# A four-layer graph network on one core: one ScalarE tile in the first groups, two sign buffers, projections one tile later, and other entries into layers 2 and 3

## The chip, the cores and the metric

The kernel runs on one core of a Trainium2 chip. A core has TensorE (PE, matmul), VectorE (DVE), ScalarE (ACT), GpSimd (POOL) and SyncE (SP), which here only issues transfers, and 16 DMA engines. The metric is the device time of one execution in microseconds; the times are medians of several runs of the same program.

## The reference

The network has 3327 nodes with 256 features and four layers, each applied as x = x + layer(relu(layernorm(x))) with a dense 3327 x 3327 matrix `adj` of which about 1% is set, the diagonal included.

```python
# layer 0, two steps n
R = S + eye; R = R / R.sum(-1)            # S = adj
A = top_p_attention(Xa, W1, W2, W3)       # softmax(q k^T), keep the largest 0.9 of each row
Xf = R @ Xf
Xa = A @ Xa
Z = Z + Xf @ U1[n].T + Xa @ U2[n].T       # at the end layernorm(X + Z)
# layer 1
filt = tanh(adj * adj) * (adj > 0)        # the 700 largest of each row
feat = relu(filt @ (tanh(h @ W_proj) @ W_gcn))
# layers 2 and 3
e = leaky_relu(Wh @ a1 + (Wh @ a2).T)     # masked by adj > 0 (layer 2: or the diagonal)
h = softmax(e) @ Wh                       # layer 3 ends in elu
```

## The kernel before, in words

The nodes are padded to 26 tiles of 128 rows. Everything is in 32-bit floats and stays on the core, apart from rows that go out to DRAM and come back.

**Layer 0** runs from 0 to about 2010 us, in two steps `s`, the second from about 1022 us. A step takes its 26 tiles in groups of three (`group`). A group makes the scores of its tiles (L1042), brings them out of PSUM on VectorE (L1016) and takes their exponentials on ScalarE (L1025). Then it looks for the threshold of the top 0.9 of each row in four rounds `r`: each round sums what lies above the present guess over the whole row of 3328 scores. A tile in `on_act` has that sum made by two ScalarE passes (L1126, Relu and Sign into the scratch tile `junk_a`), every other tile by one VectorE pass (L1131); `ON_ACT = [2, 2, 1, 2]` says how many of a group's three tiles are ScalarE's in each round. At the end of a round some ten small VectorE instructions (from L1137) make the next guess, for all three tiles at once, from both engines' sums. After the rounds each tile has three more passes (L1173, L1176, L1187). The group's tiles then go to `weighted`, which turns the kept scores with PE transposes (L951), copies them out on ScalarE (L953), multiplies them with Xa (L941), loads the tile's row of Xf as `xf_in` (L935), turns both rows (L785) and multiplies them with U1 and U2 (L971). `neighbours` makes the row R @ Xf of a tile: four blocks of the turned adjacency are loaded (`blk`, L906), in step 0 their signs are taken on ScalarE into `sg` (L909) and stored for layers 2 and 3 (`sign_d`, L910), and 26 matmuls follow (L915, two records each). Its result goes out through `xf_row` (L923, L924).

`group`, `weighted` and `neighbours` are generators. `overlapped` starts a group every 20 ticks and runs one stage of each generator per tick, so that about two groups and several tiles are in work together.

**Layer 1** (to 2343 us) goes tile by tile: two halves of the turned adjacency are loaded into one of three pairs of places, filtered on VectorE (L1478) and ScalarE (L1479), and multiplied (L1482). For the tile before, `summed` adds the result to x and takes its statistics; for the tile before that, `tile_in` makes the input of layer 2: the normed row `hr` (ScalarE, L1400), its two PE transposes (L785) with a copy `ht` (ScalarE, L786), the projection (PE, L1405) and its copies `sd` and `wh` (ScalarE, L1409 and L1410). After the last tile of a span of four, `spread` lays the source terms over all partitions (L1422, L1425) and takes maxima over the first span's positions (VectorE, L1429). Positions `pos` of the set elements are found from the rows of `adj` (L1496) and stored (`pos_d`).

**Layers 2 and 3** (`attention`, 2343 to 2731 and 2731 to 3099 us) go by spans of four tiles, the last of two. For pairs of column tiles, ScalarE makes two exponentials (L1585, L1586), VectorE combines and masks them (L1587, L1588), and PE multiplies (L1594). Statistics, `tile_in` and `spread` of the next layer stand in a list `todo`; from the second block of a span on, each block takes one entry of it. What is left after the last span is done at its end, then the next layer begins with `scores_of` (L1534, L1541).

All transfers are issued by SP in one order. The order of every engine's instructions is fixed when the program is built: it follows the order in which the code above emits them, with instructions whose operands are expected earlier moved ahead. At run time each engine takes its list in order, and an instruction at the head of it waits for its operands and for the release of the buffer that it writes. A tile with `bufs=1` has one buffer; without `bufs`, its pool's default of two.

Of the kernel before, what the change touches and what calls it, by code (L numbers as in the profile page):

```python
# [9 lines left out]
F32 = mybir.dt.float32  # L10
BF16 = mybir.dt.bfloat16
I32 = mybir.dt.int32
U8 = mybir.dt.uint8
I8 = mybir.dt.int8
AF = mybir.ActivationFunctionType
ALU = mybir.AluOpType
# [4 lines left out]
P = 128  # L21
N = 3327
NT = 26
NP = NT * P
LAST = N - (NT - 1) * P
D = 256
# [8 lines left out]
ON_ACT = [2, 2, 1, 2]  # L35
# [31 lines left out]
def kernel(  # L67
# [23 lines left out]
    nc = tc.nc  # L91
# [649 lines left out]
    spans = [list(range(i, min(i + 4, NT))) for i in range(0, NT, 4)]  # L741
# [4 lines left out]
    def layers(fast):  # L746
# [54 lines left out]
        def layer0(wp, mp, ap_, tp, sp):  # L801
# [97 lines left out]
            def neighbours(s, it, xf):  # L899
# [3 lines left out]
                for chunks in QB:  # L903
# [3 lines left out]
                    if s == 0:  # L907
                        sg = tp.tile([P, 7, P], I8, tag="sg", bufs=1, name="sg")
                        nc.scalar.activation(sg[:, :n, :], blk[:, :n, :], AF.Sign)  # L909
                        nc.sync.dma_start(sign_d[it, :, chunks[0] : chunks[0] + n, :], sg[:, :n, :])  # L910
# [16 lines left out]
            def weighted(s, it, e, norm, xa, xa_next, us):  # L927
# [3 lines left out]
                else:  # L931
                    base = tp.tile([P, D], F32, tag="base", bufs=1, name="base_row")
                    nc.sync.dma_start(base, zz_d[it * P : (it + 1) * P, :])
                xf_in = tp.tile([P, D], F32, tag="xf_in", name="xf_in")
                nc.sync.dma_start(xf_in, (xf_d, xf2_d)[s][it * P : (it + 1) * P, :])  # L935
# [65 lines left out]
            def group(s, tiles, xa, xf, xa_next, us, slots, products_of, also):  # L1001
# [113 lines left out]
                for r in range(ROUNDS):  # L1115
                    on_act = list(range(max(g - ON_ACT[r], g - 2 if g > 2 else 1), g)) if g > 1 else []
                    A = slice(on_act[0], g) if on_act else None
# [241 lines left out]
        class Entry:  # L1359
# [5 lines left out]
            def __init__(self, name, w, wh, dk_tag, eye):  # L1365
                self.w, self.wh, self.eye, self.mv = w, wh, eye, {}
                for t in wh.halves:
# [3 lines left out]
                self.dk = slot(dk_tag, [P, NP], f"dk{name}")  # L1371
                self.tops = late.tile([P, 4, len(spans)], F32, name=f"tops{name}")
                sq = late.tile([P, 2], F32, tag="sq", name="sq")
                nc.vector.tensor_tensor(sq, w[:, :, D + 1], w[:, :, D + 1], ALU.mult)
                ps = ps_row()
                nc.tensor.matmul(ps[:, :2], ones, sq, start=True, stop=True)
                self.shift = late.tile([P, 1], F32, name=f"shift{name}")
                self.low = late.tile([P, 1], F32, name=f"low{name}")
                shift = self.shift
# [5 lines left out]
                nc.gpsimd.tensor_scalar(self.low, shift, -1.0 + 2.0**-20, None, ALU.mult)  # L1385
                if not eye:

                    self.part = late.tile([P, D + 1], F32, name="part")
                    nc.gpsimd.memset(self.part, 0.0)

# [5 lines left out]

            def tile_in(self, it, src):
                hr = late.tile([P, D], F32, tag="hr", bufs=2, name="hr")
                mv = self.mv.pop(it)
                nc.scalar.activation(hr, src, AF.Relu, bias=mv[:, 0:1], scale=mv[:, 1:2])  # L1400
                ht = late.tile([P, D], F32, tag="ht", bufs=2, name="ht")
                transposed(hr, ht)
                ps = ps_row()
# [48 lines left out]
        entry2 = Entry("2", w2l, nodes(("a0", "a1"), D + 2, "wh2"), "bl", True)  # L1452
        with tc.tile_pool(name="l1", bufs=2, reuse_waits="tile") as l1:
            third = l1.tile([P, 2, HB * P], F32, bufs=1, name="blk1_2")
            places = [[places[n][:, k, :] for n in range(2)] for k in range(2)] + [[third[:, n, :] for n in range(2)]]
# [7 lines left out]

            def entered2(it):
                entry2.tile_in(it, xn(it))
                if it in ends:
                    entry2.spread(ends.index(it))

            for it in range(NT):
# [3 lines left out]
                for hb in range(2):  # L1473
                    filt = places[it % 3][hb]
                    nc.sync.dma_start(
# [9 lines left out]
                if it >= 1:  # L1485
                    summed(it - 1)
                if it >= 2:
                    entered2(it - 2)
                ar = slot(f"e{it % 2}", [P, NP], "adj_rows")
# [3 lines left out]
                for a, b in rows_to_load(it):  # L1493
                    nc.sync.dma_start(ar[a:b, :N], adj[it * P + a : it * P + b, :])
                pos = pos_first[:, it, :] if it in spans[0] else l1.tile([P, NP], U8, tag="pos", name="pos")
                nc.vector.tensor_scalar(  # L1496
# [4 lines left out]
            summed(NT - 1)  # L1501
            entered2(NT - 2)
            entered2(NT - 1)


# [10 lines left out]
        def attention(entry, finish, following=None):  # L1516
# [33 lines left out]
            for i, span in enumerate(spans):  # L1550
# [16 lines left out]
                for b, j0 in enumerate(range(0, NT, JB)):  # L1567
# [30 lines left out]
                    if 1 <= b <= len(ahead):  # L1598
# [6 lines left out]
                        if b == len(ahead):  # L1605
                            sb_next = scores_of(ahead, top)
                    if b and todo:
                        for work in todo.pop(0):
                            work()
# [10 lines left out]
                if following is not None:  # L1620

                    stats = [lambda it=it: following.stats(it, xn(it)) for it in span]
                    rest = [lambda it=it: following.tile_in(it, xn(it)) for it in span]
                    todo += [stats[:2]] + [rest[k : k + 1] + stats[k + 2 : k + 3] for k in range(n)]
                    todo.append([lambda i=i: following.spread(i)])
            for works in todo:
# [108 lines left out]
```

## Time and profile before

The median of three runs is 3104.74 us (3103.69 to 3111.75).

| | us |
|---|---|
| profiled execution, its own time | 3100.91 |
| its span | 3099.1 |
| PE busy | 2823.0 (91%) |
| PE weight loads busy | 2277.8 (73%) |
| VectorE busy | 2370.4 (76%) |
| ScalarE busy | 1979.7 (64%) |
| GpSimd busy | 417.8 (13%) |
| chain of work that ended last | DVE 38%, PE 27%, ACT 16%, issue 8%, DMA 7%, POOL 3% |

The span is the part of the execution that the profiler sees. Busy times of the engines overlap, so they don't add up to it. A line of the profile names an engine, a line of the code (L1126), and output and input; "<-" ahead of another instruction names what ended an idle time. The line numbers are those of the kernel before.

### The profile page before, as it was taken

Reading aid. Unit: us, or ns where it says so; the run is one execution under the profiler, and the core shown is the slowest. Engines: PE = TensorE matmul, PEld = TensorE weight load, DVE = VectorE, ACT = ScalarE, POOL = GpSimd, SP = SyncE. Lnnn points to the kernel's source line nnn. Section 1 sums busy time; section 2 is a strip of 40 time slices with the busy share of each in tenths; the row PEclk is TensorE's granted clock in tenths of the full one; section 3 lists DMA queues with packets and bytes.
Section 4 is the critical chain, followed back from the end, with each engine's and each line's share of the span. In section 5 each row is a group of like instructions: output and inputs, shape, how many; then the busy total and the mean of one; then the engine's idle time right before and its main releaser. Section 6 shows DMA issues by size and latency. Waiting matters only on the chain.

```text
span 3099.1 us, 37681 instructions
## 1 busy us (share of the span) xinstructions
PE 2823.0 (91%) x13454; PEld 2277.8 (73%) x13454; DVE 2370.4 (76%) x4133; ACT 1979.7 (64%) x2633; POOL 417.8 (13%) x742
## 2 busy tenths in 40 slices
PE   7788899999999899999999988999997999979998
PEld 5466677777778576667777767888886887758887
DVE  3678889778874588889876858377765999769996
ACT  6767787768773566687666555433334777657776
POOL 0120010000001001111110024211110333210000
PEclk9889999999999999999999989999998999989999
DMA  4431112321242231211232231388871211112221
GB/s 138 131 102 45 55 45 76 95 78 57 75 121 87 73 103 53 64 35 54 74 90 72 83 114 60 105 321 318 324 243 32 71 59 59 30 48 78 75 74 37
DMA packets 183035, 298.83 MB, mean 96 GB/s; under 512 B 24701, under 2 KB 137016, under 8 KB 179512
## 3 DMA queue, kind: packets, MB, share of 16 engines
q1 hardware_dynamic: 182838, 296.34, 30.3%
q8 instruction: 108, 1.77, 0.3%
q14 instruction: 89, 0.72, 0.1%
HBM read 251.97 MB, written 44.30 MB: 96 GB/s over the span
## 4 chain that ended last, share of the span: by engine, by line
DVE 38%; PE 27%; ACT 16%; issue 8%; DMA 7%; POOL 3%; SPq 0%; ACTq 0%; POOLq 0%; DVEq 0%
ACT junk_a L1126 9%; PE ps_wide L1594 5%; DVE below L1173 4%; PE ps_out L941 4%; PE ps_acc L915 4%; DVE w L1176 4%; PE ps_wide L1482 4%; DVE below L1131 3%; DVE e L1187 3%; DVE places L1601 3%; DVE places L1587 2%; DVE below L1085 2%; DVE places L1588 2%; DMA blk<-in_adj_t 2%; DMA adj_rows<-in_adj 2%
## 5 line engine op out<-in xcount | busy, mean ns | idle before, releaser
L1126 ACT ACTIVATE junk_a<-e,minus 128x3328 int8<-128x3328 f32 x208 | 638.8, 3071 | 3.7
L1594 PE MATMUL ps_wide<-wh,places 128*128 128x257 f32 x1872 | 451.2, 383 | 35.6 <-DVE places L1588 32.7
L1594 PEld LDWEIGHTS ps_wide<-wh,places 128*128 128x128 f32 x1872 | 353.3, 191 | 93.6 <-ACT places L1586 16.5
L915 PE MATMUL ps_acc<-h,blk 128*128 128x258 f32 x1352 | 333.3, 399 | 46.8 <-ACT xf_row L923 37.1
L915 PEld LDWEIGHTS ps_acc<-h,blk 128*128 128x128 f32 x1352 | 261.8, 198 | 102.3 <-ACT xf_row L923 42.7
L1016 DVE TENSOR_SCALAR_CACHE_REDUCE e<-ps_wide 128x1024 f32<-128x1024 f32 (+1 forms) x176 | 178.6, 1019 | 206.9 <-PE ps_wide L1042 206.4
L915 PE MATMUL ps_acc<-xf,blk 128*128 128x256 f32 x1352 | 312.9, 384 | 14.3 <-ACT xf_row L923 14.2
L941 PE MATMUL ps_out<-h,wt 128*128 128x256 f32 x1352 | 311.2, 381 | 4.7 <-ACT wt L953 4.7
L941 PE MATMUL ps_out<-xa,wt 128*128 128x256 f32 x1352 | 311.9, 381 | 0.9 <-ACT wt L953 0.7
L1585 ACT ACTIVATE places<-places,sd 128x512 f32<-128x512 f32 (+1 forms) x364 | 246.3, 684 | 100.5 <-PE ps_wide L1594 67.6
L1482 PE MATMUL ps_wide<-gw,blk 128*128 128x256 f32 x1352 | 300.9, 379 | 1.3 <-ACT blk L1479 1.3
L915 PEld LDWEIGHTS ps_acc<-xf,blk 128*128 128x128 f32 x1352 | 253.9, 191 | 61.8 <-ACT xf_row L923 19.3
L1482 PEld LDWEIGHTS ps_wide<-gw,blk 128*128 128x128 f32 x1352 | 254.5, 190 | 35.0 <-ACT blk L1479 1.7
L941 PEld LDWEIGHTS ps_out<-h,wt 128*128 128x128 f32 x1352 | 249.8, 190 | 40.1 <-ACT wt L953 6.3
L941 PEld LDWEIGHTS ps_out<-xa,wt 128*128 128x128 f32 x1352 | 249.4, 190 | 34.8 <-ACT wt L953 3.0
L1586 ACT ACTIVATE places<-places,d 128x512 f32<-128x512 f32 (+1 forms) x364 | 235.8, 682 | 48.7 <-DVE places L1587 48.2
L1131 DVE SCALAR_TENSOR_TENSOR below<-e,v 128x3328 f32<-128x3328 f32 x72 | 265.3, 3684 | 1.8
L1587 DVE TENSOR_TENSOR places<-places,places 128x1024 f32<-128x1024 f32 (+1 forms) x182 | 210.2, 1163 | 65.8 <-ACT places L1585 63.7
L1042 PE MATMUL ps_wide<-keys,q 64*128 64x512 f32 (+1 forms) x832 | 215.9, 570 | 17.8 <-DVE e L1016 14.8
L953 ACT COPY wt<-ps_wide 128x1024 f32<-128x1024 f32 x208 | 175.2, 846 | 86.2 <-PE ps_wide L951 85.6
L1588 DVE SCALAR_TENSOR_TENSOR places<-blk_s,places 128x1024 f32<-128x1024 int8 (+1 forms) x182 | 206.3, 1142 | 2.0
L1176 DVE MAX8 w<-below 128x8 f32<-128x3328 f32 x52 | 188.3, 3621 | 0.3
(275 smaller groups left out, 4312.6 us busy)
## 6 DMA issues: line engine op xcount, KB each, us to landing
blk<-in_adj_t SPq DMA_DIRECT2D x104, 448.0 KB, 3.5
blk<-in_adj_t SPq DMA_DIRECT2D x52, 832.0 KB, 7.1
adj_rows<-in_adj SPq DMA_DIRECT2D x25, 1663.5 KB, 8.4
blk<-in_adj_t SPq DMA_DIRECT2D x104, 384.0 KB, 3.3
blk_s<-sign_d SPq DMA_DIRECT2D x72, 256.0 KB, 2.9
blk_s<-pos_d SPq DMA_DIRECT2D x44, 416.0 KB, 3.6
pos_d<-pos SPq DMA_DIRECT2D x22, 416.0 KB, 2.9
xf_d<-xf_row SPq DMA_DIRECT2D x52, 128.0 KB, 2.4
```

What stands on the lines that cost most here:

```text
L915: nc.tensor.matmul(acc[:, :w], blk[:, j, :], xf(jc)[:, :w], start=(jc == 0), stop=(jc == NT - 1))
L941: nc.tensor.matmul(po, wt[:, k * P : (k + 1) * P], xa(jc)[:, :D], start=(jc == 0), stop=(jc == NT - 1))
L1042: nc.tensor.matmul(pl[:, f * 512 : f * 512 + cw], q[f * DA : (f + 1) * DA, :], kt[f * DA : (f + 1) * DA, s, c0 : c0 + cw], start=True, sto ...
L1126: nc.scalar.activation(junk, es[i], (AF.Relu, AF.Sign)[n], bias=minus[:, 0, i : i + 1], accum_out=(ga, sa)[n][:, 0, i : i + 1],)
L1131: nc.vector.scalar_tensor_tensor(below, es[i], v[:, 3, i : i + 1], es[i], ALU.is_ge, ALU.mult, accum_out=v[:, 1, i : i + 1],)
L1176: nc.vector.max(w9[:, i, 1:9], below)
L1482: nc.tensor.matmul(po, filt[:, j * P : (j + 1) * P], gw(jc), start=(jc == 0), stop=(jc == NT - 1))
L1585: nc.scalar.activation(e1[:, :, q, :], s0, AF.Exp, bias=sd[:, jc + q, 1:2])
L1586: nc.scalar.activation(e2[:, :, q, :], s1, AF.Exp, bias=d2[:, jc + q : jc + q + 1])
L1587: nc.vector.tensor_tensor(e1, e1, e2, ALU.max)
L1588: nc.vector.scalar_tensor_tensor(e1, signs[:, :n, j : j + 2, :], 0.0, e1, ALU.is_gt, ALU.min)
L1594: nc.tensor.matmul(pos_[k], e1[:, k, q, :], wh(jc + q)[:, : D + 1], start=(jc + q == 0), stop=(eye and jc + q == NT - 1),)
```

## The change

1. `sg` gets two buffers, `xf_in` one instead of two.
2. In the group that holds tile 0, which is the first of each step, one tile is ScalarE's in every round instead of `ON_ACT[r]`.
3. The bound `shift` of an `Entry` is no longer computed when the entry is made but by `shifted`, called in the third tile of layer 1 and in the second span of layer 2.
4. `tile_in` becomes `turned` (norm, transposes, copy) and `projected` (matmul and copies, `spread` after it); in both callers `projected` comes one tile later than `turned`. At the end of layer 1 the last tiles are made with less distance from the sum that they follow.
5. In `attention`, the last span takes two entries of `todo` in every block, the first included.
6. In layer 1 the three pairs of places are taken in turn from the second on, and the two `pos` tiles are named and chosen by `it % 2`.

```diff
@@ -905,7 +905,7 @@
                     blk = ap_.tile([P, 7, P], F32, tag="blk", name="blk")
                     nc.sync.dma_start(blk[:, :n, :], adj_t[it, :, chunks[0] : chunks[0] + n, :])
                     if s == 0:
-                        sg = tp.tile([P, 7, P], I8, tag="sg", bufs=1, name="sg")
+                        sg = tp.tile([P, 7, P], I8, tag="sg", name="sg")
                         nc.scalar.activation(sg[:, :n, :], blk[:, :n, :], AF.Sign)
                         nc.sync.dma_start(sign_d[it, :, chunks[0] : chunks[0] + n, :], sg[:, :n, :])
                     if it in chunks:
@@ -931,7 +931,7 @@
                 else:
                     base = tp.tile([P, D], F32, tag="base", bufs=1, name="base_row")
                     nc.sync.dma_start(base, zz_d[it * P : (it + 1) * P, :])
-                xf_in = tp.tile([P, D], F32, tag="xf_in", name="xf_in")
+                xf_in = tp.tile([P, D], F32, tag="xf_in", bufs=1, name="xf_in")
                 nc.sync.dma_start(xf_in, (xf_d, xf2_d)[s][it * P : (it + 1) * P, :])
                 po = ps_out0()[:, :D]
 
@@ -1113,7 +1113,9 @@
                 todo = list(products_of)
                 first = 2 if g == len(todo) else 0
                 for r in range(ROUNDS):
-                    on_act = list(range(max(g - ON_ACT[r], g - 2 if g > 2 else 1), g)) if g > 1 else []
+
+                    most = 1 if tiles[0] == 0 else ON_ACT[r]
+                    on_act = list(range(max(g - most, g - 2 if g > 2 else 1), g)) if g > 1 else []
                     A = slice(on_act[0], g) if on_act else None
                     if on_act:
                         nc.scalar.mul(minus[:, 0, A], v[:, 3, A], -1.0)
@@ -1363,19 +1365,25 @@
 
 
             def __init__(self, name, w, wh, dk_tag, eye):
-                self.w, self.wh, self.eye, self.mv = w, wh, eye, {}
+                self.w, self.wh, self.eye, self.mv, self.ht = w, wh, eye, {}, {}
                 for t in wh.halves:
                     nc.gpsimd.memset(t[:, :, D : D + 1], 1.0)
                 self.sd = late.tile([P, NT, 2], F32, name=f"sd{name}")
                 self.d2 = late.tile([P, NT], F32, name=f"d2{name}")
                 self.dk = slot(dk_tag, [P, NP], f"dk{name}")
                 self.tops = late.tile([P, 4, len(spans)], F32, name=f"tops{name}")
+                self.shift = late.tile([P, 1], F32, name=f"shift{name}")
+                self.low = late.tile([P, 1], F32, name=f"low{name}")
+                if not eye:
+
+                    self.part = late.tile([P, D + 1], F32, name="part")
+                    nc.gpsimd.memset(self.part, 0.0)
+
+            def shifted(self):
                 sq = late.tile([P, 2], F32, tag="sq", name="sq")
-                nc.vector.tensor_tensor(sq, w[:, :, D + 1], w[:, :, D + 1], ALU.mult)
+                nc.vector.tensor_tensor(sq, self.w[:, :, D + 1], self.w[:, :, D + 1], ALU.mult)
                 ps = ps_row()
                 nc.tensor.matmul(ps[:, :2], ones, sq, start=True, stop=True)
-                self.shift = late.tile([P, 1], F32, name=f"shift{name}")
-                self.low = late.tile([P, 1], F32, name=f"low{name}")
                 shift = self.shift
                 nc.vector.tensor_reduce(shift, ps[:, :2], AX.X, ALU.add)
                 nc.gpsimd.tensor_scalar(shift, shift, 1.01 * D, EPS, ALU.mult, ALU.add)
@@ -1383,10 +1391,6 @@
                 nc.gpsimd.tensor_scalar(shift, shift, 1.0, None, ALU.add)
 
                 nc.gpsimd.tensor_scalar(self.low, shift, -1.0 + 2.0**-20, None, ALU.mult)
-                if not eye:
-
-                    self.part = late.tile([P, D + 1], F32, name="part")
-                    nc.gpsimd.memset(self.part, 0.0)
 
             def stats(self, it, src):
 
@@ -1394,12 +1398,15 @@
                 nc.gpsimd.tensor_scalar(mv[:, 0:1], mv[:, 0:1], mv[:, 1:2], -1.0, ALU.mult, ALU.mult)
                 self.mv[it] = mv
 
-            def tile_in(self, it, src):
+            def turned(self, it, src):
                 hr = late.tile([P, D], F32, tag="hr", bufs=2, name="hr")
                 mv = self.mv.pop(it)
                 nc.scalar.activation(hr, src, AF.Relu, bias=mv[:, 0:1], scale=mv[:, 1:2])
-                ht = late.tile([P, D], F32, tag="ht", bufs=2, name="ht")
-                transposed(hr, ht)
+                self.ht[it] = late.tile([P, D], F32, tag="ht", bufs=2, name="ht")
+                transposed(hr, self.ht[it])
+
+            def projected(self, it):
+                ht = self.ht.pop(it)
                 ps = ps_row()
                 for c in range(2):
                     nc.tensor.matmul(
@@ -1451,6 +1458,8 @@
         places = [slot(f"e{4 + n}", [P, 2, HB * P], f"blk1_{n}") for n in range(2)]
         entry2 = Entry("2", w2l, nodes(("a0", "a1"), D + 2, "wh2"), "bl", True)
         with tc.tile_pool(name="l1", bufs=2, reuse_waits="tile") as l1:
+
+            pos_places = [l1.tile([P, NP], U8, bufs=1, name=f"pos{n}") for n in range(2)]
             third = l1.tile([P, 2, HB * P], F32, bufs=1, name="blk1_2")
             places = [[places[n][:, k, :] for n in range(2)] for k in range(2)] + [[third[:, n, :] for n in range(2)]]
             po_of = {}
@@ -1461,8 +1470,8 @@
                 nc.vector.scalar_tensor_tensor(xn(it), pre, 0.0, xs(it), ALU.max, ALU.add)
                 entry2.stats(it, xn(it))
 
-            def entered2(it):
-                entry2.tile_in(it, xn(it))
+            def projected(it):
+                entry2.projected(it)
                 if it in ends:
                     entry2.spread(ends.index(it))
 
@@ -1471,7 +1480,7 @@
                     po2 = ps_wide()
                 po = po_of[it] = po2[:, 512 * (it % 2) : 512 * (it % 2) + D]
                 for hb in range(2):
-                    filt = places[it % 3][hb]
+                    filt = places[(it + 1) % 3][hb]
                     nc.sync.dma_start(
                         filt, adj_t[it, :, hb * HB : (hb + 1) * HB, :].rearrange("p j i -> p (j i)")
                     )
@@ -1484,23 +1493,31 @@
                         )
                 if it >= 1:
                     summed(it - 1)
-                if it >= 2:
-                    entered2(it - 2)
+
+                for k in range(it - 2 if it < NT - 1 else it - 1, it - 1 if it < NT - 2 else it):
+                    if k >= 0:
+                        entry2.turned(k, xn(k))
+                if it == 2:
+                    entry2.shifted()
+                for k in range(it - 3 if it < NT - 1 else it - 2, it - 2 if it < NT - 2 else it - 1):
+                    if k >= 0:
+                        projected(k)
                 ar = slot(f"e{it % 2}", [P, NP], "adj_rows")
                 r = rows_of(it)
                 if r < P:
                     nc.vector.memset(ar, 0.0)
                 for a, b in rows_to_load(it):
                     nc.sync.dma_start(ar[a:b, :N], adj[it * P + a : it * P + b, :])
-                pos = pos_first[:, it, :] if it in spans[0] else l1.tile([P, NP], U8, tag="pos", name="pos")
+                pos = pos_first[:, it, :] if it in spans[0] else pos_places[it % 2]
                 nc.vector.tensor_scalar(
                     pos[:, :N], ar[:, :N], 0.0, None, ALU.is_gt, ALU.add, accum_out=counts[:, it : it + 1]
                 )
                 nc.gpsimd.memset(pos[:, N:], 0)
                 nc.sync.dma_start(pos_d[it], pos)
             summed(NT - 1)
-            entered2(NT - 2)
-            entered2(NT - 1)
+            projected(NT - 2)
+            entry2.turned(NT - 1, xn(NT - 1))
+            projected(NT - 1)
 
 
         att = fast.enter_context(tc.tile_pool(name="att", bufs=1, reuse_waits="tile"))
@@ -1604,8 +1621,10 @@
                         )
                         if b == len(ahead):
                             sb_next = scores_of(ahead, top)
-                    if b and todo:
-                        for work in todo.pop(0):
+                    if following is not None and (i, b) == (1, 1):
+                        following.shifted()
+                    for _ in range(2 if ahead == [] else 1 if b else 0):
+                        for work in todo.pop(0) if todo else []:
                             work()
                 for k, it in enumerate(span):
                     if not eye:
@@ -1620,9 +1639,12 @@
                 if following is not None:
 
                     stats = [lambda it=it: following.stats(it, xn(it)) for it in span]
-                    rest = [lambda it=it: following.tile_in(it, xn(it)) for it in span]
-                    todo += [stats[:2]] + [rest[k : k + 1] + stats[k + 2 : k + 3] for k in range(n)]
-                    todo.append([lambda i=i: following.spread(i)])
+                    turned = [lambda it=it: following.turned(it, xn(it)) for it in span]
+                    made = [lambda it=it: following.projected(it) for it in span]
+                    todo += [stats[:2]] + [
+                        turned[k : k + 1] + made[max(k - 1, 0) : k] + stats[k + 2 : k + 3] for k in range(n)
+                    ]
+                    todo.append(made[-1:] + [lambda i=i: following.spread(i)])
             for works in todo:
                 for work in works:
                     work()
```

## The prediction

> **What bounds the kernel now.** I read the page's engine totals, then busy time by stretches, then the waits of the stretches that are not full, and last the timeline around each place that the diff touches.
>
> ```profile
> PE 2823.0 (91%) x13454; PEld 2277.8 (73%) x13454; DVE 2370.4 (76%) x4133; ACT 1979.7 (64%) x2633; POOL 417.8 (13%) x742
> ```
>
> TensorE's matmul work is the same before and after the change, so at an unchanged clock (mean 0.973) a gain can come only out of its 3099.1 - 2823.0 = 276 us of idle time. Where that idle time lies is seen in stretches: width, then busy us of PE, weight loads, DVE, ACT and POOL, then PE's clock, the DMA share and GB/s.
>
> ```profile
> 100.00:150.00 50.00, 36.99 (x142) 26.83 (x141) 24.07 (x76) 40.63 (x34) 8.97 (x16) 0.86 0.52 151
> 150.00:200.00 50.00, 34.58 (x138) 27.90 (x138) 37.71 (x62) 28.77 (x27) 19.94 (x15) 0.83 0.49 147
> 250.00:300.00 50.00, 41.63 (x197) 31.44 (x196) 37.96 (x89) 34.50 (x38) 1.63 (x10) 0.93 0.17 49
> 1050.00:1100.00 50.00, 44.12 (x189) 33.65 (x187) 32.18 (x91) 42.21 (x33) 3.14 (x8) 0.93 0.42 119
> 2010.00:2343.00 333.00, 319.85 (x1507) 276.19 (x1506) 226.87 (x265) 111.86 (x154) 53.24 (x109) 1.00 0.79 288
> ```
>
> From 100 to 200 PE idles 28.4 us, from 1050 to 1100 it idles 5.9; layer 1 (2010 to 2343) has 13.2 us. At both starts of layer 0's steps ACT is the busiest engine after PE, and DVE has room. The timeline of DVE in the first group's second round shows why (start, duration, and in brackets the idle time before it):
>
> ```profile
> 133.02 3.69 DVE L1131 SCALAR_TENSOR_TENSOR below<-e,v 128x3328 f32<-128x3328 f32 x1
> ...
> 148.08 0.16 DVE L1137 SCALAR_TENSOR_TENSOR sa<-sa,v 128x2 f32<-128x2 f32 x1 [10.77 <-ACT junk_a L1126]
> ...
> 150.38 3.69 DVE L1131 SCALAR_TENSOR_TENSOR below<-e,v 128x3328 f32<-128x3328 f32 x1
> ```
>
> DVE makes one pass over one tile and then waits 10.8 us for ACT, which makes two passes for each of two tiles. The waits of the whole run, and those of PE within layer 1, hold the two other targets (total us, times, longest):
>
> ```profile
> ACT sg L909 <- DMA sign_d<-sg: 54.9, 23, 5.4
> SPq L935 <- PE ps_row L785: 152.7, 28, 18.0
> ```
>
> ```profile
> PE ps_row L1405 <- ACT ht L786: 10.6, 10, 2.6
> PE ps_row L1422 <- ACT sd L1409: 1.3, 1, 1.3
> PE ps_wide L1482 <- ACT blk L1479: 1.3, 1, 1.3
> ```
>
> **What the Trainium skill says.** "Perfetto Trace Analysis", Optimization Strategy: look for the gaps on the engine that should be saturated, stretch by stretch; repeated equal gaps can mean too few buffers. The trace agrees as to layer 1 (ten like gaps), though their cause is an order, not a buffer. "ScalarE: Activation LUTs", What ACT_TABLE_LOAD costs: an ACTIVATE with a pointer bias takes about 280 ns + 0.833 ns an element; for 3328 that is 3.05 us, and the trace has 3.07. So ACT's pair costs 2 x (3.07 + 0.19 read) = 6.5 us a tile, DVE's one pass 3.69 + 0.08. "TensorE: Matmul & The Clock Gate", What's actually happening: an array idle for some 3.4 us falls to half clock. Agreed: the four records of the projection L1405 take 2.09 us at 2350.76, after a gap, and 1.14 in the shadow at 2344.01.
>
> **Part 1, one ACT tile in the first group of each step.** Of rounds r0, r1, r3 one tile goes from ACT to DVE: ACT loses 3 x 6.5 = 19.5 us, DVE gains 3 x 3.8 = 11.3. Round r2 has that split already and is the price. In step 0 the rounds last 26.2, 17.4, 9.9 and 17.2 us (starts of L1131 at 106.8, 133.0, 150.4, 160.3, end 177.5); r1 and r3 fall to about 9.9, r0, held by the exponentials of its third tile, by some 5: 7.4 + 7.3 + 5 = 20 us. In step 1 they last 18.0, 15.9, 9.1, 15.4: r0 gives some 3 (DVE waits there for PE's L1042 until 1069.1, and for ACT only 2.6), so 6.8 + 6.3 + 3 = 16 us. The first weighted products start that much sooner. But PE doesn't save it all: in the built order, of the neighbour products (L915, rows of 333.3 and 312.9 us, so 646.2 / 52 = 12.4 us a tile) 6.3 tiles stood before the first weighted tile and now 5.0; in step 1 32.3 and now 31.2. So 1.3 x 12.4 = 16 and 1.1 x 12.4 = 14 us of PE work move behind it and are caught up after nine more weighted tiles. From 200 to 500 PE idles 28.6 us (by 50 us: 4.9, 8.4, 2.9, 6.7, 2.9, 2.8) and can take some of it for nothing. I let 40% of the moved work be hidden: -20 + 0.6 x 16 = **-10.4** in step 0, -16 + 0.6 x 14 = **-7.6** in step 1. Ends: all hidden -20 and -16, none -4 and -2. The cover of DVE's added 11 us is its waits for ACT (6.3, 10.8 and 2.3 us in r0, r1, r3 of step 0, the last one beside 8.6 us more ended by PE); without it 11 us a step would come back.
>
> **Part 2, two sign buffers, one xf_in.** The second sg buffer takes away up to 54.9 us of ACT waits, 18.3 of these between 60 and 200 us. PE waits for blk copies through POOL there (4.7 us), else hardly at all: **-2**, ends 0 and -5. The single xf_in makes each load (L935, 2.0 us to landing, 3.8 at most) wait for the transpose (L785) of the tile before instead of the one before that. The load moves one tile later in SP's list, so SP stands at the same release as now (152.7 us over 28 loads), and neighbour blocks, q and base loads behind it are held no longer. Transposes of successive tiles are at 563.8, 611.9, 636.7, 669.2, 716.6: at least 24.8 us apart, against 2.0 + SP's 5.5 mean wait. **0**, ends 0 and +8 (a miss of 3.8 us at a couple of tiles).
>
> **Part 3, projection one tile after the transpose in layers 1 and 2.** In layer 1, PE's 10.6 us behind ht copies go, since PE now uses the copy of the tile before. Next could be DMA: 2 x 832 + 1663.5 + 416 KB a tile is 3.83 MB per 333/26 = 12.8 us, 299 GB/s, and the page reaches 324, good for 11.8 us; DVE (68% busy) isn't near. **-8**, ends 0 and -10.6. With the step its ACT copies (sd L1409 0.16, wh L1410 0.38, dk L1425 0.69 us) and, for a span's last tile, L1422 and four L1429 passes on DVE also come a tile later; none of them has a reader before attention starts. It issues no DMA. In layer 2's attention PE waits 3.9 us for ht; DVE, the bound there (PE waits 17.0 us for its L1588), keeps half: **-2**, ends 0 and -4. The order of the pos and filter buffers and the moved shift chain (one 0.59 us matmul, L1376, and a few small DVE and POOL ones) are hidden by the matmul stretch into which they go: **0**, and +3 if layer 1's first filter load were late.
>
> **Part 4, the two entries.** PE's timeline between layers 1 and 2:
>
> ```profile
> 2343.09 0.38 PE L785 MATMUL ps_row<-ident,hr 128*128 128x128 f32 x2
> 2344.01 1.14 PE L1405 MATMUL ps_row<-w2l,ht 128*128 128x258 f32 x4 [0.53 <-ACT ht L786]
> 2344.98 0.73 PE L1422 MATMUL ps_row<-ident,sd 128*128 128x128 f32 x4
> 2349.13 0.44 PE L785 MATMUL ps_row<-ident,hr 128*128 128x128 f32 x2 [3.41 <-ACT hr L1400]
> 2350.76 2.09 PE L1405 MATMUL ps_row<-w2l,ht 128*128 128x258 f32 x4 [1.19 <-ACT ht L786]
> 2352.64 0.63 PE L785 MATMUL ps_row<-ident,hr 128*128 128x128 f32 x2
> ```
>
> Tile 23's projection and spread run in the shadow of tile 24's statistics. In the new order they stand behind tile 24's transpose at 2349.13: 2.09 cold + 0.73 to 1.5, in place of the 1.19 us wait for ht, so tile 24's projection starts at about 2352.3, not 2350.8; tile 25's wait of 0.53 goes. **+1.5**, ends 0 and +3. Between layers 2 and 3 the spread of the sixth span leaves the tail: four L1429 passes from 2732.15 to 2734.60, 2.5 us on DVE ahead of the statistics, and about 0.6 us of ht waits. Against that, two works a block in the last span put transposes and projections close together on PE, which may wait for ACT copies of 0.4 to 1.2 us there, 1 to 3 in all: **-1**, ends -3 and +2.
>
> **Sum.** -10.4 - 7.6 - 2 + 0 - 8 - 2 + 0 + 1.5 - 1 = -29.5 us. The profiled execution took 3100.9 us (span 3099.1 and 1.8 around it), 3.8 below the median of 3104.7. I take the difference to the median: **3075 us**.
>
> **Rivals.** *A, the start gain is handed back*: PE is the bound from 200 on (46 to 48 of 50), all the moved neighbour tiles are paid for: -4 - 2 at the starts, -1 for the sign buffer, -5 in layer 1 and nothing at the entries: 3104.7 - 12 = about 3093. For it: the 95% PE of 500 to 1000 (473.9 of 500); against it: 200 to 450. *B, no measurable change*: layer 1 is held by DMA at a share of 0.79 (0.74 to 0.88) so that its gaps reappear as waits for filters, and A as well: -8 + 1.5, with +2 to +6 at small places, 3100 to 3104. *C, slower*: the one xf_in buffer holds SP's in-order list. If a load waits longer than now, the neighbour blocks behind it come late, and PE's L915 starves. 29.5 us over 52 loads is 0.57 us, and it decides from there on; at 1 us a load the sum is -29.5 + 52 = +22, 3127. For it: SP waits up to 18.0 us at this line already; against it: the 24.8 us spacing and the load's later place. *D, the change does nothing at the start*, because r0 is bound by the third tile's exponentials: its gain is only 5 of 20, so this costs no more than A.
>
> **Chances.** Forecast 0.63 (its own range 3056 to 3088), A 0.15, B and smaller sums 0.12, C 0.10. The forecast and A are faster, with a few of C's mild cases and B's better ones in the middle: faster by more than 0.3% (9 us, about what a measurement of this kernel tells from none) 0.77, within 0.13, slower 0.10. For 8 in 10 the range takes the forecast down to all-hidden starts, A, and part of B: 3053 to 3103.
>
> **What would show it.** First group of step 0: DVE's idle before L1137 for ACT falls from 10.8 to under 1, rounds of about 10 us, the first L951 some 20 us earlier; step 0's end earlier by half of that. ACT's sg wait near 0; SP's wait at L935 about 150. In layer 1, no PE wait for ht, and a stretch of 325 instead of 333. Transition gaps of 27.4 (2343.3 to 2370.7) and 30 us (2730.5 to 2760.6) become 29 and 29. It is wrong if PE waits for neighbour blocks more than now, if DVE's wait moves to L1016 in rounds, or if PE's granted clock drops below 0.97 as it fills up.

## The result, and the profile after

The changed kernel takes 3089.28 us (median of 7 runs, 3087.01 to 3094.23), the kernel before beside it 3104.8 (7 runs, 3101.63 to 3111.75). The ratio is 0.9946, its 95% interval [0.9935, 0.9956] (given in brackets from here on): about 16 us faster, where 29.5 had been forecast. The same program, taken once more in the last set of experiments, gave 3096.72 (6 runs, 3084.47 to 3097.98) and 0.9969 [0.9953, 0.9985]. The two intervals share only gains of 13.7 to 14.6 us, and between the two sets of runs the size is 8 to 16 us: it is known no better than that.

The engine totals of the changed kernel:

```profile
span 3086.7 us, 37714 instructions
PE 2824.4 (92%) x13454; PEld 2287.4 (74%) x13454; DVE 2394.5 (78%) x4145; ACT 1942.3 (63%) x2609; POOL 400.4 (13%) x742
```

ScalarE has lost 37 us and VectorE gained 24, while PE's work is as it was. The span is 12.4 us shorter than that of the kernel before. The stretches, with the columns as in the prediction:

```profile
100.00:150.00 50.00, 35.57 (x136) 25.81 (x135) 48.31 (x100) 37.81 (x34) 19.83 (x15) 0.84 0.44 134
250.00:300.00 50.00, 44.81 (x234) 36.62 (x235) 49.17 (x89) 35.40 (x38) 1.45 (x7) 1.00 0.24 70
1990.00:2330.00 340.00, 326.26 (x1517) 283.02 (x1515) 227.37 (x265) 111.10 (x155) 47.18 (x111) 0.98 0.76 277
```

From 100 to 150 VectorE goes from 24 to 48 us busy, and from 250 to 300 PE gains 3.2: that is the first group ready sooner. But layer 1, given here by 340 us within it, idles 13.7 us of PE, as before, and its clock is 0.98 instead of 1.00. The timeline of VectorE in the first group's second round (L1133 and L1139 are the old L1131 and L1137):

```profile
121.86 3.69 DVE L1133 SCALAR_TENSOR_TENSOR below<-e,v 128x3328 f32<-128x3328 f32 x1
...
125.88 3.67 DVE L1133 SCALAR_TENSOR_TENSOR below<-e,v 128x3328 f32<-128x3328 f32 x1
...
131.35 0.15 DVE L1139 SCALAR_TENSOR_TENSOR sa<-sa,v 128x1 f32<-128x1 f32 x1
```

The wait of 10.8 us is gone, and the next round starts 11.3 us after this one instead of 17.4. PE's waits in layer 1, of the changed kernel:

```profile
PE ps_row L1429 <- ACT sd L1416: 7.2, 3, 3.5
PE ps_row L1429 <- ACT ht L786: 4.9, 2, 3.1
```

The waits for ht at the projection (10.6 us) are gone too. In their place PE stands 12.1 us at the spread's transposes (L1429, L1422 in the kernel before), which had cost 1.3. Of the other lines of the changed kernel, L1404 is the norm `hr`, L1412 the projection, L1416 its copy `sd`, L1487 and L1488 the filter passes of VectorE and ScalarE (the latter a Tanh), and L1491 the filter matmuls.

By parts, from marks in the two traces (start of the last tile's U product in each step of layer 0, first and last filter matmul of layer 1, first and last matmul of each attention):

| us | before | after | difference | forecast |
|---|---|---|---|---|
| layer 0, end of step 0 | 1019.4 | 1008.0 | -11.4 | -10.4, and -2 for sign waits |
| layer 0, step 1 | 981.6 | 974.7 | -6.9 | -7.6 |
| layer 1 | 344.5 | 349.1 | +4.6 | -8 |
| to layer 2 | 27.4 | 26.2 | -1.2 | +1.5 |
| layer 2 | 360.0 | 365.7 | +5.7 | -2 |
| to layer 3 | 29.9 | 26.2 | -3.7 | -1 |
| layer 3 | 328.3 | 328.2 | 0 | 0 |

One trace of each is not enough to trust single rows. The experiments each left a trace of one more execution, and the means over them come below.

### The profile page after: what moved, and what is told of

Same layout as the page of the kernel before. It is cut to its first block, busy times and chain, and to the rows that moved or that the text cites. A ratio compares the mean times of both kernels' runs of the same rounds, so it can differ in the third digit from the quotient of the medians.

```text
span 3086.7 us, 37714 instructions
## 1 busy us (share of the span) xinstructions
PE 2824.4 (92%) x13454; PEld 2287.4 (74%) x13454; DVE 2394.5 (78%) x4145; ACT 1942.3 (63%) x2609; POOL 400.4 (13%) x742
## 4 chain that ended last, share of the span: by engine, by line
DVE 30%; PE 25%; ACT 10%; issue 7%; DMA 5%; POOL 2%; SPq 0%; ACTq 0%; DVEq 0%; POOLq 0%
PE ps_wide L1611 6%; ACT junk_a L1128 5%; PE ps_out L941 4%; PE ps_acc L915 4%; PE ps_wide L1491 3%; DMA adj_rows<-in_adj 3%; DVE below L1175 3%; DVE w L1178 3%; DVE places L1618 3%; DVE places L1604 2%; DVE below L1133 2%; DVE places L1605 2%; DVE e L1189 2%; DVE below L1085 2%; DMA blk<-in_adj_t 1%
## 5 line engine op out<-in xcount | busy, mean ns | idle before, releaser
L1128 ACT ACTIVATE junk_a<-e,minus 128x3328 int8<-128x3328 f32 x196 | 602.0, 3071 | 4.1
L1491 PE MATMUL ps_wide<-gw,blk 128*128 128x256 f32 x1352 | 302.6, 384 | 0.8 <-ACT gw L1302 0.7
L1133 DVE SCALAR_TENSOR_TENSOR below<-e,v 128x3328 f32<-128x3328 f32 x78 | 287.7, 3689 | 1.9
L1491 PEld LDWEIGHTS ps_wide<-gw,blk 128*128 128x128 f32 x1352 | 259.5, 193 | 37.5 <-ACT gw L1302 1.1
```

The costliest lines, as they stand in the source:

```text
L1128: nc.scalar.activation(junk, es[i], (AF.Relu, AF.Sign)[n], bias=minus[:, 0, i : i + 1], accum_out=(ga, sa)[n][:, 0, i : i + 1],)
L1133: nc.vector.scalar_tensor_tensor(below, es[i], v[:, 3, i : i + 1], es[i], ALU.is_ge, ALU.mult, accum_out=v[:, 1, i : i + 1],)
L1491: nc.tensor.matmul(po, filt[:, j * P : (j + 1) * P], gw(jc), start=(jc == 0), stop=(jc == NT - 1))
```

## The experiments

**The first group alone.** The kernel before, with

```diff
-                    on_act = list(range(max(g - ON_ACT[r], g - 2 if g > 2 else 1), g)) if g > 1 else []
+                    most = 1 if tiles[0] == 0 else ON_ACT[r]
+                    on_act = list(range(max(g - most, g - 2 if g > 2 else 1), g)) if g > 1 else []
```

> The kernel before with one edit: one ScalarE tile in all rounds of the first group of each step. Theory (the start gain is this edit's alone, and the sign and xf_in buffers give nothing): step 0 ends about 11 us earlier and step 1 gains 7 more, so layer 1 starts near 1981 instead of 1998.8; the rest is as before; about 3087 us, 18 below before. Rival (the second sign buffer carries part of it): step 0 gains only 6 to 8 and the whole 12, about 3093 us.

It took 3098.02 us, ratio 0.9976 [0.9967, 0.9984]: 7.6 less than before by the medians, below what both theories said. In its trace layer 1 starts at 1985.5 instead of 1998.8, 13.3 us sooner, with step 1 at 974.7 as in the changed kernel; but layer 1 then takes 351.8 us, with 14.1 us of waits for ht, one of them of 4.2. So the edit gives layer 0 most of its gain, and a layer whose code is untouched differs by 7 us from one execution to another.

**The buffers alone.**

```diff
-                        sg = tp.tile([P, 7, P], I8, tag="sg", bufs=1, name="sg")
+                        sg = tp.tile([P, 7, P], I8, tag="sg", name="sg")
...
-                xf_in = tp.tile([P, D], F32, tag="xf_in", name="xf_in")
+                xf_in = tp.tile([P, D], F32, tag="xf_in", bufs=1, name="xf_in")
```

> The kernel before with two sign buffers and one xf_in buffer alone. Theory: nothing that can be measured, 3100 to 3106 us, ScalarE's wait for sign stores near 0, SP's wait at the xf_in load about 150 us as before. Rival (SP held up by the one xf_in buffer): 3110 us or more, with longer waits at that load. Rival of the other sign (sign waits were on the path): 3097 us or less.

3104.24 us, ratio 1.0001 [0.9992, 1.001]. ScalarE's waits for sign stores fall from 54.9 to 1.5 us. But its waits for the loaded block, ahead of the same instruction, grow. Before:

```profile
ACT sg L909 <- DMA blk<-in_adj_t: 58.1, 25, 8.4
```

With the two edits:

```profile
ACT sg L909 <- DMA blk<-in_adj_t: 89.3, 44, 6.5
ACT sg L909 <- DMA sign_d<-sg: 1.5, 1, 1.5
```

The time stays: step 0 ends at 1020.9 and step 1 takes 981.5, as before. Most of the wait moved to the load, and what went was on no path. SP's wait at the xf_in load did not stay near 150 us, as both the prediction and the theory had it, but grew from 152.7 to 222.4; that cost no time that can be measured. The two buffers were changed together, so a gain of one and a cost of the other, each within some 3 us, are not told apart.

**Projection ahead of the next transposes.** The changed kernel, with the order of the two calls exchanged in layer 1 up to its last two tiles (`turns` holds the loop that calls `turned`):

```diff
+                if it >= NT - 2:
+                    turns()
                 if it == 2:
                     entry2.shifted()
                 for k in range(it - 3 if it < NT - 1 else it - 2, it - 2 if it < NT - 2 else it - 1):
                     if k >= 0:
                         projected(k)
+                if it < NT - 2:
+                    turns()
```

> The changed kernel, but in layer 1, up to its last two tiles, the projection and spread of a tile are made before the next tile's transposes, not after them. Theory (the spread's transposes wait for the PSUM buffer of the transposes just before them, whose copy to ht stands behind Tanh in ScalarE's list): PE's waits at the spread fall from 12.1 to 1 to 4 us, the three half-clock stretches in layer 1 go, and layer 1 takes 337 to 341 us instead of 349; about 3079 us in all. Rival (layer 1 is held by its transfers): the waits come back at the matmuls L1491 for their filter, layer 1 stays at 345 to 349, 3087 to 3089 us.

3088.46 us, ratio 0.9953 [0.9935, 0.9972], which can't be told from the changed kernel. The spread's waits fall only to 9.1 us, one of them 4.4. Layer 1 takes 342.4 us. The theory is not borne out; nor is the rival, since the filter matmuls wait 0.6 us in all.

**One entry a block in the last span of layer 2.**

```diff
-                    for _ in range(2 if ahead == [] else 1 if b else 0):
+                    for _ in range(1 if b else 0):
```

> The changed kernel with one entry of the list per block in the last span of layer 2, from the second block on, as in the kernel before. Theory (the two entries a block only carry work from behind the last span into it): the last span takes 31 to 32 us instead of 35.1, the gap after it 29 to 30 instead of 26.2; 3087 to 3091 us. Rival (it is a gain, since the last span's waits have another cause): 3092 to 3094 us.

3090.96 us, ratio 0.9956 [0.9936, 0.9976]. The last span, counted from the last products of the span ahead of it, goes from 35.1 back to 30.5 us, and the gap after it from 26.2 to 28.0, both below what the theory said: layer 2 and gap together 389.2 against 391.9. The work moved from the gap into the span and gained nothing on the way. Layer 1, which is as in the changed kernel, took 342.9 us here, with 9.0 us of waits at the spread.

**The spread in a bank of its own.**

```diff
-                    entry2.spread(ends.index(it))
+                    entry2.spread(ends.index(it), ps_out0)
...
-                pb = ps_spread()
+                pb = (bank or ps_spread)()
```

> The changed kernel, with the spread of layer 1 in a PSUM bank of its own (the one that layer 0 used for its weighted sums) instead of one of the two that transposes and projections take in turn. Theory (the spread's first transposes wait for that bank): PE's waits at the spread in layer 1, 9 to 12 us in the changed kernel, fall to 1 to 4, which are waits for sd alone; layer 1 takes 338 to 342 us. Rival (they wait for sd, which stands behind Tanh on ScalarE): 7 us or more remain at the fourth transposes.

3085.88 us, ratio 0.9938 [0.9921, 0.9954]. My theory fell: the waits are still there, now all for sd, and layer 1 takes 345.7 us.

```profile
PE ps_out L1429 <- ACT sd L1416: 13.5, 5, 3.8
```

**The spread one tile later, in the bank that it had.**

```diff
             def projected(it):
                 entry2.projected(it)
-                if it in ends:
-                    entry2.spread(ends.index(it))
+                for k in (it - 1, it) if it == NT - 1 else (it - 1,):
+                    if k in ends:
+                        entry2.spread(ends.index(k))
```

> The changed kernel with the spread of layer 1 one tile later than the projection, in the PSUM bank that it had. Theory (the waits at the spread were for sd behind Tanh, and a tile's distance removes them): waits at the spread below 3 us in layer 1, layer 1 336 to 341 us, total 3078 to 3084. Rival (the spread's first transposes still wait for the copy of the transposes just before them, which hold their bank): 7 us or more stay, 3086 to 3089 us.

3086.15 us, ratio 0.9951 [0.9934, 0.9967]. Here the rival is right about the wait and the total; layer 1 takes 341.9 us, just above what the theory said:

```profile
PE ps_row L1429 <- ACT ht L786: 8.3, 2, 5.3
```

**Both of these diffs together**, first with the one entry a block of the diff above, then with two:

> The changed kernel with the spread of layer 1 in its own PSUM bank and one tile later than the projection, and one entry per block in the last span of layer 2. Theory (after this nothing in layer 1 has PE waiting on ScalarE): no wait above 0.3 us at spread or projection, no half clock, layer 1 335 to 339 us, 3078 to 3082 us in all. Rival (transfers set layer 1): matmuls L1491 wait for their filter in place of it, layer 1 343 or more, 3086 to 3090 us.

> As the changed kernel with the late spread in its own bank, but with two entries a block in the last span of layer 2, as in the changed kernel. Theory (these two entries neither gain nor lose): layer 2 and the gap after it together 390 to 392 us, the total within 3 us of the one with one entry, 3076 to 3082. Rival (they cost 3): 3082 to 3085.

With one entry 3078.79 us, ratio 0.9913 [0.9891, 0.9935]; with two 3081.74, ratio 0.9928 [0.9912, 0.9945]: both faster than the kernel before, and by their intervals not to be told apart. Against the changed kernel the medians are 8 to 10 us lower; beside its repeat on the same chip (3084.47 to 3097.98) the one with two entries ran in 3079.04 to 3083.78. Layer 1 takes 336.7 and 341.8 us. Neither the spread nor the projection waits any more. Half clock has not gone, as the theory had it: the clock records show 3.4 us of it with one entry and 10.2 with two, each time at a wait for hr. Of PE's waits in layer 1 with one entry, all but 1.8 us are these:

```profile
PE ps_row L785 <- ACT hr L1404: 6.0, 2, 5.3
```

So two releases lay one behind the other: sd, and the PSUM bank (a part of the memory that PE writes) that the copy to ht gives back. Both are ScalarE copies that stand in its list with the Tanh of the next filter. Taking away one left the other (13.5 us, 8.3 us), and only without both do the spread's waits go. The changed kernel's ScalarE around the longest wait but one:

```profile
2074.60 1.59 ACT L1488 ACTIVATE blk<-blk 128x1664 f32<-128x1664 f32 x1 [4.75 <-DVE blk L1487]
2076.09 0.37 ACT L786 ACTIVATE ht<-ps_row 128x256 f32<-128x256 f32 x1
2076.40 1.59 ACT L1488 ACTIVATE blk<-blk 128x1664 f32<-128x1664 f32 x1
2077.89 0.14 ACT L1416 COPY sd<-ps_row 128x2 f32<-128x2 f32 x1
```

PE had transposed and projected by 2073.4, so from then on both copies could have been made. ScalarE, idle for 4.75 us until 2074.60, made neither, because at the head of its list was a Tanh whose filter pass VectorE had still to make; sd came last, after a second Tanh. VectorE made its position pass L1512 first, and that one had waited for its rows of `adj`:

```profile
2069.13 3.62 DVE L1512 TENSOR_SCALAR_CACHE_REDUCE pos<-adj_rows 128x3327 uint8<-128x3327 f32 x1 [2.00 <-DMA adj_rows<-in_adj]
2072.68 0.08 DVE L1512 DVE_READ_ACCUMULATOR pos<-adj_rows 128x1 f32 x1
2072.68 3.69 DVE L1487 SCALAR_TENSOR_TENSOR blk<-blk 128x1664 f32<-128x1664 f32 x2
```

Freed of its wait for ht, the projection comes at once after the next tile's transposes, and so the spread comes sooner to copies that, as read at this place, may be several microseconds late; how late depends here on when a transfer lands. What is left without either, one wait of 5.3 us for hr with one entry and two of 8.1 us together with two, may have the same source; that is not shown. Around the one of 5.3 us two loads of `adj` rows took 14.5 us in the median, against 8.5 over the run of the changed kernel.

**Layers 1 to 3 alone, and layer 0 alone.** The changed kernel with the diffs of the first two experiments reversed, and the kernel before with both.

> The changed kernel with layer 0 as before: ScalarE tiles, sign and xf_in buffers. Theory (layers 1 to 3 give almost nothing, since the waits for ht in layer 1 came back at the spread): 3101 to 3105 us. Rival (layer 0 gives only the 8 us that its first group alone gave, and the rest comes from here): 3096 to 3099 us.

> The kernel before with the edits of layer 0 alone: one ScalarE tile in the first groups, two sign buffers, one xf_in buffer. Theory (layer 0 carries the result): step 0 ends 8 to 11 us earlier, step 1 gains 7 more, 3088 to 3092 us. Rival (as the first group alone): 3096 to 3100 us, with the rest of the 15.5 us coming from layers 1 to 3.

Layers 1 to 3 alone: 3105.73 us, ratio 1.0004 [0.9992, 1.0015]. They give nothing that can be measured. Layer 0 alone: 3094.44 us, ratio 0.9967 [0.9952, 0.9981], a gain of 10 us; the time is just above what its theory said and below its rival's, and by the intervals not to be told apart from the first group alone. Layer 1 starts at 1987.3 in its trace, but step 0 ends only 4.2 us earlier than in the trace of before, for 8 to 11 expected.

**The sixth span's spread out of the shadow.** The kernel before, at the end of layer 1:

```diff
             def entered2(it):
                 entry2.tile_in(it, xn(it))
-                if it in ends:
+                if it in ends and it < NT - 3:
                     entry2.spread(ends.index(it))
...
             entered2(NT - 2)
+            entry2.spread(ends.index(NT - 3))
             entered2(NT - 1)
+            entry2.spread(ends.index(NT - 1))
```

> The kernel before, but at the end of layer 1 the sixth span's spread stands behind tile 24's projection. Theory (the spread's VectorE passes beside the statistics slow them on GpSimd, so the shadow was not free): tile 24's norm on ScalarE starts 3.9 us after the last matmul instead of 5.2, and the gap before layer 2 is 25.5 to 27 instead of 27.4; all else as before, 3103 to 3106 us. Rival (the order on PE is what counts): the norm starts at 5.2 as before and the gap is 28 to 29.5.

3102.53 us, ratio 0.9999 [0.9989, 1.0009], with the gap ahead of layer 2 at 26.33 us instead of 27.43, and tile 24's norm (2344.22) 3.9 us after the last matmul (2340.3) instead of 5.2: the theory's numbers. GpSimd's steps of the statistics in the kernel before, while VectorE makes the spread's passes from 2346.47 on:

```profile
2346.60 0.65 POOL L793 TENSOR_SCALAR mv_a<-mv_a 128x1 f32<-128x1 f32 x1
2347.34 1.10 POOL L1394 TENSOR_SCALAR mv_a<-mv_a 128x1 f32<-128x1 f32 x1
2348.40 1.03 POOL L794 TENSOR_TENSOR mv_a<-mv_a,minus_half 128x1 f32<-128x1 f32 x1
```

The same steps with the spread behind:

```profile
2343.60 0.22 POOL L793 TENSOR_SCALAR mv_a<-mv_a 128x1 f32<-128x1 f32 x1
2343.92 0.27 POOL L1394 TENSOR_SCALAR mv_a<-mv_a 128x1 f32<-128x1 f32 x1
2344.14 0.57 POOL L794 TENSOR_TENSOR mv_a<-mv_a,minus_half 128x1 f32<-128x1 f32 x1
```

The Trainium skill, "SBUF — State Buffer", Who interferes with whom, says that a VectorE instruction with two SBUF inputs contends with a GpSimd instruction that reads SBUF. The spread's passes have two, and the steps of 0.22, 0.27 and 0.57 us take 0.65, 1.10 and 1.03 beside them. That an SBUF port is the reason is the page's word, and the traces agree with it. In all 14 of them these steps on `mv_a` take at most 0.26 us (L793), 0.60 (L794) and 0.27 (L1394) wherever no VectorE instruction, or one with a single tensor operand, runs beside them; the longer ones all stand beside VectorE instructions with two, the spread's passes among them.

**The changed kernel once more.**

> The changed kernel once more, beside these. Theory (one profile of layer 1 carries chance of some 5 us from late transfers): layer 1 anywhere from 343 to 350 us, PE's waits at the spread 9 to 13, total 3087 to 3091. Rival (349 us is its length): 348 to 350 again.

3096.72 us, as said above, more than the 3087 to 3091 expected, and layer 1 took 349.7 us: the rival's number. Yet in the experiment with one entry, with the same layer 1, it took 342.9.

**Means over the traces.** Mean length by the code that a trace has, in us, with the traces' own values where they scatter:

| | as before | as changed | difference |
|---|---|---|---|
| end of step 0 | 1019.2 (3 traces, 1017.6 to 1020.5) | 1011.5 (9, 1007.8 to 1015.8) | -7.7 |
| step 1 | 980.4 (3) | 974.8 (9) | -5.6 |
| layer 1 | 346.9 (344.5, 345.3, 345.4, 347.7, 351.8) | 347.9 (342.9, 349.1, 349.7, 350.0) | +1.0 |
| to layer 2 | 27.4 (4) | 25.5 (4) | -1.9 |
| layer 2 | 361.0 (5) | 365.5 (7) | +4.5 |
| to layer 3 | 29.9 (5) | 26.2 (7) | -3.7 |

They add up to -13.4 us, inside the second interval (-4.7 to -14.6 us) and just outside the first (-13.7 to -20.2). The gain lies in layer 0 alone; the other parts cancel.

## Why the prediction was right or wrong

It was right in direction and in its range (3089.28 in 3053 to 3103), and about half of the forecast gain came, in the repeat about a quarter. The range was wide, and the parts did not come as forecast. The time lies nearer to rival A (about 3093) than to the forecast, but A had all the moved work paid for, -6 us in layer 0, and -5 in layer 1. By the means layer 0 gave -13.3 and layer 1 nothing: that A's sum is near is luck.

**Part 1: right in mechanism, too large by some 5 us.** In the trace that came with the result the first weighted transposes (L951) start at 175.4 instead of 197.2, 22 us sooner, for 20 forecast. But that execution of before was the latest of three. In the mean of the traces in the table they start at 194.4 (192.6 to 197.2) in the code as before and at 177.7 (174.0 to 181.2) as changed: 16.7 us sooner. The rest of step 0 then takes 9.1 us longer (833.9 instead of 824.8), in which PE is busy 14.3 us more and idle 5.2 less. That is 0.57 of the 16 us of moved work, for 0.6 forecast. So the hidden share was right in step 0, and the mis-sized term is the start: 20 us, read from one trace, measures 16.7. In step 1 it is the other way round. The first weighted transposes come 97.6 us after the end of step 0 instead of 113.5, 15.9 sooner, for 16; the rest takes 10.4 us longer (877.2 instead of 866.8), with PE busy 11.6 more and idle only 1.3 less. Of the 14 us about a quarter is hidden, not 40%: there PE's idle time took up less of it. In the trace that came with the result both steps looked nearly exact (-11.4 and -6.9), by chance of that execution.

**Part 2: the end that was 0.** I took -2 for the sign waits; the buffers alone gave a ratio of 1.0001. For xf_in the 0 held, and so rival C fell, but not for the reason given: SP does not stand "at the same release as now" but longer (152.7 us before, 197.5 in the changed kernel, 222.4 with the buffers alone). What it holds up cost nothing that can be measured. PE's waits for neighbour blocks, a sign that the prediction named, did grow from 0.9 to 6.9 us for the loads, while those for POOL's copies fell from 8.7 to 0.4.

**Part 3: the step that failed.** "PE's 10.6 us behind ht copies go" is right: there is not one such wait left at the projection. "Next could be DMA" is where the working went wrong. I looked for the next bound among engines and transfers and counted out of the way the instructions that come with the step: "none of them has a reader before attention starts". The spread reads sd at once, and needs a PSUM bank. Both hang on ScalarE copies behind a Tanh, and PE, in order, stands there with the filter matmuls behind it: 9 to 14 us of waits in five places. So -8 came out as +1.0. The waits are also few and long. By the clock records of the trace, those of 3.15 and 3.5 us were followed by 3.4 us of half clock each, and a third stretch of 6.8 us came at the wait of 2.4. PE's idle time in layer 1 is as in the profiled execution of before (15.0 and 14.8 us), but its busy time is 334.1 us instead of 329.7, and that execution had no half clock there. Over all traces, layer 1 as before has 0 to 6.8 us of half clock, as changed 13.7 in three of four and 6.8 in the fourth, the one of 342.9 us. With the two releases taken out of the way layer 1 took 336.7 and 341.8, some 7.6 us below the mean of before: about the forecast gain, had the spread been given a tile's distance and a bank of its own. Rival B had the right outcome for this layer with the wrong place: with the changed layer 1, the matmuls L1491 waited at most 1.2 us in all.

In layer 2 I took -2. The projection's waits for ht (4.3 us) went as well, but the spread's transposes, which had waited for nothing there, now wait 4.4 us, most of it for sd: the same exchange as in layer 1.

```profile
PE ps_row L1429 <- ACT sd L1416: 3.3, 3, 1.3
```

The layer is longer by 4.5, the larger part of it in the last span.

**Part 4: a sign wrong, the sum nearly right by luck.** I took +1.5 for the entry to layer 2, since tile 23's projection and spread no longer run in the shadow of (that is, beside) tile 24's statistics. They did stand where I put them, but the shadow was not free: the spread's passes slowed GpSimd's statistics, and tile 24's norm now starts 1.4 us sooner after the last matmul (3.85 instead of 5.23). PE also got to full clock sooner: the last projection takes 1.14 us instead of 2.09. Result -1.9. For the entry to layer 3 I took -1, out of -3.1 in the gap and +2 in the span. They were -3.7 in the gap and about +4 in the span (35.1 against 31.4): the packing costs about twice what I allowed, and the gain in the gap is near what I had. Both entries and layer 2 together were to give -1.5 and gave -1.1, because the errors cancel.

**The sum against its base.** I added to the median, rightly as it turned out: the profiled execution of before was below it in layer 1 and layer 2, and others with the same code were up to 7 us longer there.

## What to carry to other kernels

When a wait is taken away by moving a consumer one step later, list what follows the moved instruction on the same engine and what releases each of these, buffers included: the next in line may hang on the same late engine. Where two releases stand one behind the other, removing either alone leaves waits on the other, and only the pair tells. A gain at the start of a pipeline is worth the start less that part of the deferred work which later idle time doesn't hide; and a single trace can be off by as much as the effect, in its start as well as in its sum.

## What the runs showed of the hardware that was not expected

- GpSimd's small steps grow from 0.22, 0.27 and 0.57 us to 0.65, 1.10 and 1.03 while VectorE makes passes with two SBUF operands; with these passes moved behind them, the gap between two layers was 1.1 us shorter.
- Half clock, in stretches of 3.4 or 6.8 us, came in layer 1 at waits of PE as short as 3.15 and 2.4 us, less than the some 3.4 that the prediction named; with the code as before it came at one and the same wait of 2.6 us in four executions, and not in a fifth.
- One execution to another, with unchanged code, layer 1 took 344.5 to 351.8 us at a DMA share near 0.8, and step 0 with its edits ended at 1007.8 to 1015.8, while step 1 with its edits stayed within 974.2 to 975.4 and layer 3 within 328.2 to 328.3. Why one scatters and the other doesn't is not shown.
